# Pairwise products with a projected right factor: pairs ordered by right field, projections in a ring, stores of 100 pairs

## The chip, the cores and the metric

The kernel runs on one core of a Trainium2 chip. The metric is the device time of one execution in microseconds (us), the median of several runs. All transfers between the chip's main memory and the core's on-chip memory (SBUF, 128 partitions) are carried by 16 DMA engines, which take their work from queues: here one fed by the SyncE sequencer (SP) and one fed by the ScalarE sequencer (ACT). TensorE (PE) multiplies matrices into PSUM, ScalarE copies from PSUM to SBUF, VectorE (DVE) does elementwise arithmetic.

## The reference

For a batch of 4096 rows with 32 fields of 64 numbers each, every field is projected by the matrix W, and for each pair of fields i < j the left field is multiplied elementwise with the projected right field. There are 32 x 31 / 2 = 496 pairs, all in fp32:

```python
def _L0_rec_ref(x, W):                      # x (4096, 32, 64), W (64, 64)
    vid = jnp.einsum('bfd,de->bfe', x, W)
    idx_i, idx_j = jnp.triu_indices(32, k=1)
    return x[:, idx_i, :] * vid[:, idx_j, :]   # (4096, 496, 64)
```

The input is 33.6 MB and the output 520 MB, so the output is nearly all of the traffic.

## The kernel before

**Tiles.** The host lays x out as 16 tiles of 128 partitions x 32 fields x 128 numbers. A partition is one of the 64 embedding positions of one of two halves of the batch; the 128 numbers are batch rows. One field of one partition is 512 B, and one pair of one tile is 128 x 512 B = 64 KB of output.

**Loads.** W is loaded twice, onto partitions 0 to 63 and 64 to 127, by two transfers on ACT's queue (L53, L54). x of tile 0 comes in four pieces of 8 fields, last fields first, and x of tile 1 in two pieces of 16 fields, all on SP's queue (L99 to L102; the transfer itself is L61). Later tiles are loaded in four pieces of 8 fields on ACT's queue, one after each of the second to fifth chunks of the tile before (L124, L125). There are two buffers for x, so a load of tile t + 1 waits for the last product of tile t - 1.

**Projection.** `project` (L63) runs over the four groups of 8 fields. Each group takes four fp32 matmul calls of 64 x 64 by 64 x 512 (L72), which come out as eight matmul instructions in the trace, into one of four PSUM buffers, and ScalarE copies the group into `vid` (L79). `vid` is one buffer for all 32 fields of a tile; there are two of them.

**Products and stores.** Pairs are numbered by left field: `off[i]` is the first pair of left field i. The 496 pairs of a tile are cut into chunks of SLOT = 83 pairs (six a tile, the last of 81), each in one of three output buffers. `products` (L82) writes a chunk with one VectorE multiply for each left field in it (L88): the left operand is field i of x, repeated over the right fields; the right operand is a range of `vid`. `store` (L96) then sends the chunk on SP's queue. In tile 0 the chunks run backwards, from the last pair, because the last left fields need only the last fields of `vid`; its first chunk is stored in four parts (10, 18, 27 and 26 pairs) and the others in two (L107 to L117). From tile 1 on each chunk is one store (L119 to L123).

**Order.** SP's instructions stand in the order of the program text. The instructions of the other engines are ordered by the scheduler and wait for each other through semaphores. An output buffer is written again only after its store has landed on all 16 DMA engines.

Of the kernel before, what the change touches and what calls it, by code (L numbers as in the profile page):

```python
# [1 line left out]

# [4 lines left out]

F32 = mybir.dt.float32
ALU = mybir.AluOpType

P = 128

C = 128


@with_exitstack
def pairwise_bilinear_kernel(
    ctx: ExitStack,
    tc: tile.TileContext,
    x: bass.AP,  # L20
    w: bass.AP,
    out: bass.AP,
):

    nc = tc.nc
    NT, _, F, _ = x.shape
    D = P // 2
    NP = F * (F - 1) // 2

    GRP = 8  # L30
    NGRP = F // GRP
    BANK = 512 // C

    SLOT = 83
    AHEAD = 2
    PIECES = 4

    off = [i * (F - 1) - i * (i - 1) // 2 for i in range(F)]


    ctx.enter_context(tc.manual_schedule(engines={mybir.EngineType.SP}))

    const = ctx.enter_context(tc.tile_pool(name="const", bufs=1))
    xpool = ctx.enter_context(tc.tile_pool(name="x", bufs=AHEAD))
    vpool = ctx.enter_context(tc.tile_pool(name="vid", bufs=2))
    opool = ctx.enter_context(tc.tile_pool(name="out", bufs=3))
    psum = ctx.enter_context(
        tc.tile_pool(name="ps", bufs=4, space=bass.MemoryType.PSUM)
    )


    w2 = const.tile([P, D], F32)
    nc.scalar.dma_start(out=w2[0:D, :], in_=w)  # L53
    nc.scalar.dma_start(out=w2[D : 2 * D, :], in_=w)  # L54

    xs = {}

    def load(t, lo, hi, queue=nc.sync):
        if t not in xs:
            xs[t] = xpool.tile([P, F, C], F32, tag="x", name=f"x_{t}")  # L60
        queue.dma_start(out=xs[t][:, lo:hi, :], in_=x[t][:, lo:hi, :])  # L61

    def project(t, order):  # L63

        vid = vpool.tile([P, F, C], F32, tag="vid", name=f"vid_{t}")
        for g in order:
            pv = psum.tile([P, GRP, C], F32, tag="pv", name=f"pv_{t}_{g}")
            for b in range(0, GRP, BANK):
                f = g * GRP + b
                for h in range(2):  # L70
                    half = slice(h * D, (h + 1) * D)
                    nc.tensor.matmul(  # L72
                        pv[half, b : b + BANK, :],
                        lhsT=w2[half, :],
                        rhs=xs[t][half, f : f + BANK, :],
                        start=True,
                        stop=True,
                    )
            nc.scalar.copy(vid[:, g * GRP : (g + 1) * GRP, :], pv)  # L79
        return vid  # L80

    def products(t, vid, ot, base, a, b, backwards=False):  # L82

        fields = [i for i in range(F - 1) if off[i] < b and off[i + 1] > a]
        for i in reversed(fields) if backwards else fields:
            s, e = max(a, off[i]), min(b, off[i + 1])
            j = i + 1 + s - off[i]
            nc.vector.tensor_tensor(  # L88
                ot[:, s - base : e - base, :],
                xs[t][:, i : i + 1, :].to_broadcast([P, e - s, C]),  # L90
                vid[:, j : j + e - s, :],
                ALU.mult,
            )

    def store(t, ot, base, a, b):
        nc.sync.dma_start(out=out[t][:, a:b, :], in_=ot[:, a - base : b - base, :])  # L96


    for g in reversed(range(NGRP)):  # L99
        load(0, g * GRP, (g + 1) * GRP)  # L100
    load(1, F // 2, F)
    load(1, 0, F // 2)  # L102

    for t in range(NT):
        vid = project(t, reversed(range(NGRP)) if t == 0 else range(NGRP))
        bases = list(range(0, NP, SLOT))
        if t == 0:  # L107

            ends = [NP, off[27], off[24], off[21], bases[-1]]
            for n, base in enumerate(reversed(bases)):  # L110
                top = min(base + SLOT, NP)
                if n:
                    ends = [top, (base + top) // 2, base]
                ot = opool.tile([P, SLOT, C], F32, tag="o", name=f"o_{t}_{n}")
                for b, a in zip(ends, ends[1:]):
                    products(t, vid, ot, base, a, b, backwards=True)
                    store(t, ot, base, a, b)  # L117
        else:
            for n, base in enumerate(bases):  # L119
                top = min(base + SLOT, NP)  # L120
                ot = opool.tile([P, SLOT, C], F32, tag="o", name=f"o_{t}_{n}")
                products(t, vid, ot, base, base, top)
                store(t, ot, base, base, top)  # L123
                if 1 <= n <= PIECES and t + 1 < NT and t + 1 not in (0, 1):  # L124
                    load(t + 1, (n - 1) * F // PIECES, n * F // PIECES, nc.scalar)  # L125


_INS = ["r_x", "L0_rec_W"]
_OUTS = [((4096, 496, 64), "float32")]


# [28 lines left out]
```

## Time and profile before

| | |
|---|---|
| median of 3 runs (lowest, highest) | 1298.11 us (1298.02, 1298.69) |
| the profiled execution, its own time | 1297.79 us |
| its span, first to last instruction | 1295.9 us |
| VectorE busy, instructions | 1105.9 us (85%), 581 |
| TensorE busy | 219.4 us (17%) |
| ScalarE busy | 66.1 us (5%) |
| DMA packets, bytes, mean rate over the span | 24077, 553.82 MB, 427 GB/s |
| stores of 83 pairs: number, issue to landing | 75, 28.9 us |
| stores of 81 pairs | 15, 27.6 us |
| x loads of 512 KB on ACT's queue | 56, 31.8 us |
| first product of VectorE starts at | 10.89 us |
| first store is issued at | 12.6 us |

How to read it: a profile page divides the span into 40 slices and gives for each the busy share of every engine and of the DMA engines, then each DMA queue's packets, bytes and the time its packets took as a share of all 16 DMA engines' time. A packet here is one partition's contiguous piece of a transfer. The chain of waits goes back from the last instruction, at each step to what released it. "Landing" is the arrival of a transfer's completion at its semaphore. Each transfer adds one to its semaphore from each of the 16 DMA engines, so the trace also has the moment at which each engine finished its part.

### The profile page before, as it was taken

The page shows a single profiled execution, that of the slowest core. Times are in us where ns is not written, and L with a number is a line of the kernel's source. Part 1 is how long each engine was busy: PE and PEld are TensorE (multiplying, and loading weights), DVE is VectorE, ACT ScalarE, POOL GpSimd, SP SyncE. Part 2 cuts the span into 40 slices and gives each one's busy share as a digit, 9 for nine tenths or more (in the row PEclk, how much of TensorE's full clock was granted, in tenths as well). Part 3 has the DMA queues.
Part 4 walks back from the last instruction along what each step waited for, and adds up shares of the span by engine and source line. Part 5 has one row for each costly group of instructions (what it writes and reads, how often), then busy time and mean ns, then how long its engine had stood idle before and what let it go on. Part 6 is the DMA issues. An engine that isn't in the chain of part 4 may idle for free.

```text
span 1295.9 us, 2185 instructions
## 1 busy us (share of the span) xinstructions
PE 219.4 (17%) x512; PEld 55.2 (4%) x512; DVE 1105.9 (85%) x581; ACT 66.1 (5%) x65; POOL 0.2 (0%) x4
## 2 busy tenths in 40 slices
PE   5013022120221302113031120211203122021000
PEld 2000000000000000000000000000000000000000
DVE  6999988889888888888888888888888888888991
ACT  2001000000000000000000000000000000000000
POOL 0000000000000000000000000000000000000000
PEclk9556556565665556655566555655556555565555
DMA  8999999999999999999999999999999999999998
GB/s 337 430 403 442 433 434 432 430 434 431 431 435 435 431 432 434 433 430 435 432 432 436 432 429 432 433 431 431 434 428 431 439 427 438 430 423 444 430 430 353
DMA packets 24077, 553.82 MB, mean 427 GB/s; under 512 B 2817, under 2 KB 2817, under 8 KB 10625
## 3 DMA queue, kind: packets, MB, share of 16 engines
q1 hardware_dynamic: 15840, 524.30, 93.9%
q10 hardware_dynamic: 8224, 29.40, 5.6%
q8 instruction: 4, 0.07, 0.0%
q14 instruction: 9, 0.07, 0.0%
HBM read 33.59 MB, written 520.09 MB: 427 GB/s over the span
## 4 chain that ended last, share of the span: by engine, by line
DMA 63%; DVE 33%; issue 1%; PE 0%; DVEq 0%; ACT 0%
DMA out_dram<-o 63%; DVE o L88 33%; DMA w<-in_L_rec_W_dram 0%; PE pv L72 0%; DVEq L154 0%; ACT vid L79 0%; DVEq L88 0%
## 5 line engine op out<-in xcount | busy, mean ns | idle before, releaser
L88 DVE TENSOR_TENSOR o<-x,vid 128x1408 f32<-128x1408 f32 (+15 forms) x581 | 1105.9, 1974 | 163.7 <-DMA out_dram<-o 152.9
L72 PE MATMUL pv<-x,w 64*64 64x512 f32 x512 | 219.4, 1002 | 958.4 <-DMA x<-in_r_x_dram 953.1
L79 ACT COPY vid<-pv 128x1024 f32<-128x1024 f32 x64 | 64.8, 1012 | 1110.8 <-PE pv L72 1072.2
L72 PEld LDWEIGHTS pv<-x,w 64*64 64x64 f32 x512 | 55.2, 205 | 1120.9 <-issue 1109.1
L79 ACT ACT_TABLE_LOAD x1 | 1.3, 1283 | 2.0 <-issue 2.0
L139 POOL MEMSET const-bfloat16-1.0<- 128x1 bf16 x1 | 0.1, 101 | 0.0
L139 POOL MEMSET const-uint8-127<- 128x1 uint8 x1 | 0.1, 101 | 0.0
L139 POOL MEMSET const-float32-0.0<- 128x1 f32 x1 | 0.1, 98 | 0.2 <-issue 0.2
L139 POOL MEMSET const-float32-1.0<- 128x1 f32 x1 | 0.1, 98 | 0.0
## 6 DMA issues: line engine op xcount, KB each, us to landing
out_dram<-o SPq DMA_DIRECT2D x75, 5312.0 KB, 28.9
out_dram<-o SPq DMA_DIRECT2D x15, 5184.0 KB, 27.6
x<-in_r_x_dram ACTq DMA_DIRECT2D x56, 512.0 KB, 31.8
out_dram<-o SPq DMA_DIRECT2D x5, 2688.0 KB, 10.2
out_dram<-o SPq DMA_DIRECT2D x5, 2624.0 KB, 10.8
x<-in_r_x_dram SPq DMA_DIRECT2D x4, 512.0 KB, 5.8
x<-in_r_x_dram SPq DMA_DIRECT2D x2, 1024.0 KB, 9.8
out_dram<-o SPq DMA_DIRECT2D x1, 1728.0 KB, 5.5
```

Of the source, the lines that this page charges most:

```text
L72: nc.tensor.matmul(pv[half, b : b + BANK, :], lhsT=w2[half, :], rhs=xs[t][half, f : f + BANK, :], start=True, stop=True,)
L79: nc.scalar.copy(vid[:, g * GRP : (g + 1) * GRP, :], pv)
L88: nc.vector.tensor_tensor(ot[:, s - base : e - base, :], xs[t][:, i : i + 1, :].to_broadcast([P, e - s, C]), vid[:, j : j + e - s, :], ALU ...
L139: nc = _bacc.Bacc("TRN2", target_bir_lowering=False, num_devices=1)
```

## The change

The pairs of a tile are numbered by right field: pair (i, j) is number `first(j) + i` with `first(j) = j (j - 1) / 2`. The outer loop runs over the right field j, and one multiply takes a range of left fields of x and the one projected field j, repeated. The host puts the output's pairs back into the reference's order. A slot holds 100 pairs instead of 83 (five a tile, the last of 96), still with three buffers. `vid` is now one tile per group of 8 fields, in a ring of three buffers, instead of two whole buffers. The scratch space for software-made DMA descriptors is reduced to 1024.

Stores of the first two tiles end where the list GROWING says, and at the end of each slot and tile; after it is used up, each slot is one store. Pairs begin with right field 1 in every tile, so the first products need the first fields, and x of tile 0 is loaded first fields first.

W comes from the host stacked twice, in one transfer, and is the first one on SP's queue. x of tile 0 is loaded in four pieces as before and every later tile in two pieces of 16 fields (8 KB a partition), tiles 0 and 1 on SP and the others on ACT; the load of tile t + 1 stands in the program before the projection of tile t. On ACT it comes to stand behind the copies of groups 0 and 1 of tile t and before those of groups 2 and 3.

```diff
+SLOT = 100
+
+GROWING = [
+    15, 13, 8, 19, 23, 22, 20, 16, 17, 18, 29, 31, 22, 23, 24, 25,
+    53, 22, 35, 61, 55, 45, 71, 29, 76, 24,
+]
+
+def first(j):
+    return j * (j - 1) // 2
...
-    SLOT = 83
-    AHEAD = 2
-    PIECES = 4
...
-    vpool = ctx.enter_context(tc.tile_pool(name="vid", bufs=2))
+    vpool = ctx.enter_context(tc.tile_pool(name="vid", bufs=3))
...
-    nc.scalar.dma_start(out=w2[0:D, :], in_=w)
-    nc.scalar.dma_start(out=w2[D : 2 * D, :], in_=w)
+    nc.sync.dma_start(out=w2, in_=w)
...
+    def load(t, pieces, queue):
+        xt = xpool.tile([P, F, C], F32, tag="x", name=f"x_{t}")
+        n = F // pieces
+        for lo in range(0, F, n):
+            queue.dma_start(out=xt[:, lo : lo + n, :], in_=x[t][:, lo : lo + n, :])
+        return xt
...
+    loaded = [load(0, 4, nc.sync), load(1, 2, nc.sync)]
...
+    for t in range(NT):
+        if 0 < t < NT - 1:
+            loaded.append(load(t + 1, 2, nc.scalar))
+        xt = loaded[t]
...
+            vid.append(vpool.tile([P, GRP, C], F32, tag="vid", name=f"vid_{t}_{g}"))
+            nc.scalar.copy(vid[-1], pv)
...
+        sent = 0
+        for j in range(1, F):
+            i = 0
+            while i < j:
+                at = first(j) + i
+                base = at - at % SLOT
+                if at == base:
+                    ot = opool.tile([P, SLOT, C], F32, tag="o", name=f"o_{t}_{at}")
+                n = min(j - i, base + SLOT - at)
+                nc.vector.tensor_tensor(
+                    ot[:, at - base : at - base + n, :],
+                    xt[:, i : i + n, :],
+                    vid[j // GRP][:, j % GRP : j % GRP + 1, :].to_broadcast([P, n, C]),
+                    ALU.mult,
+                )
+                i += n
+                at += n
+                if t * NP + at == until or at in (base + SLOT, NP):
+                    nc.sync.dma_start(
+                        out=out[t][:, sent:at, :],
+                        in_=ot[:, sent - base : at - base, :],
+                    )
+                    sent = at
+                    if t * NP + at == until:
+                        until += next(growing, NT * NP)
```

## The prediction

> **What bounds the kernel now.** I read the page's slices, queues and chain shares first, then the chain of waits in order of time, then windows over both ends of the span. From the page:
>
> ```profile
> DMA  8999999999999999999999999999999999999998
> ...
> q1 hardware_dynamic: 15840, 524.30, 93.9%
> q10 hardware_dynamic: 8224, 29.40, 5.6%
> ...
> DMA 63%; DVE 33%; issue 1%; PE 0%; DVEq 0%; ACT 0%
> ```
>
> The 16 DMA engines are full in all but the first and last slice. VectorE shows in the chain, but only in turns with a store it waited for. The chain of waits (start, length):
>
> ```profile
> 0.74 4.58 DMA w<-in_L_rec_W_dram
> 5.37 4.45 PE pv L72 x9
> 9.84 1.02 ACT vid L79
> 10.89 13.73 DVE o L88 x15
> ...
> 1102.15 11.79 DVE o L88 x13
> 1113.96 27.52 DMA out_dram<-o
> 1141.58 11.51 DVE o L88 x5
> 1153.11 28.97 DMA out_dram<-o
> 1182.17 11.80 DVE o L88 x13
> ```
>
> A slot comes free, VectorE refills it in 11.5 to 11.8 us, and its store needs 26 to 29 us to land because two others are ahead of it. So the DMA always has work, and one tile takes 1182.17 - 1102.15 = 80.0 us (80.2 on average from 299.48 to 1182.17). Windows (length, five engines' busy time, clock, DMA share, GB/s) show where it has none:
>
> ```profile
> 2.00:3.00 1.00, 0.00 (x0) 0.00 (x0) 0.00 (x0) 1.00 (x1) 0.00 (x0) 1.00 0.87 205
> 3.00:4.00 1.00, 0.00 (x0) 0.00 (x0) 0.00 (x0) 0.24 (x1) 0.00 (x0) 1.00 0.85 226
> ...
> 13.00:14.00 1.00, 1.00 (x7) 0.46 (x4) 1.00 (x2) 0.73 (x1) 0.00 (x0) 1.00 0.74 304
> ...
> 15.00:16.00 1.00, 1.00 (x6) 0.40 (x4) 1.00 (x2) 1.00 (x1) 0.00 (x0) 1.00 0.05 15
> ...
> 18.00:19.00 1.00, 1.00 (x6) 0.40 (x4) 1.00 (x2) 0.58 (x1) 0.00 (x0) 1.00 0.71 295
> 19.00:20.00 1.00, 1.00 (x8) 0.53 (x6) 1.00 (x1) 0.44 (x1) 0.00 (x0) 1.00 0.49 207
> ...
> 28.00:30.00 2.00, 0.00 (x0) 0.00 (x0) 2.00 (x3) 0.00 (x0) 0.00 (x0) 0.50 0.41 172
> ...
> 90.00:100.00 10.00, 5.43 (x13) 1.44 (x15) 10.00 (x5) 1.01 (x1) 0.00 (x0) 0.50 1.03 394
> ```
>
> Against 432 GB/s, the rate of most slices, the loss is: 2.9 us before 4.0, 1 - 304/432 = 0.3 at 13, 1.0 at 15, 0.3 + 0.5 at 18 to 20, 2 x 0.6 = 1.2 at 28 to 30 (3.3 us of gaps between first stores; 3.4 when summed from the single packets), and about 1.2 from 80 to 100. The end loses more: the DMA rate drops to 207 GB/s from 1288 and to 41 by 1291, because the 16 engines do not finish together. By the completion counts of the last store the first is done at 1288.9 and the last at 1295.1; on the first big stores this spread was 1.3 us.
>
> **What the skill says.** The Trainium skill's "DMA: Bandwidth & Descriptors", section "Where 436 GB/s comes from", puts the ceiling at 435.2 GB/s; the packets below give 435. Its section "Issuing engines are not separate DMA queues" says that transfers from ACT and SP share the same 16 engines and interleave; the trace agrees, since a 512 KB load takes 31.8 us to land among stores and 5.8 us at the start. "VectorE: DVE Perf Modes", section "Mode 1x (REGULAR)", gives one result a cycle for fp32 with two tensor operands; the trace has 4291 ns for 3968 elements. "TensorE: Matmul & The Clock Gate", Part 1, has matmuls at half speed for about 3.4 us; here they start 0.43 us apart until about 9.2 and 0.215 after, 3.8 us in.
>
> **The price of a packet.** The two queue rows give two equations: q1 0.939 x 16 x 1295.9 = 19470 us for 524.30 MB in 15840 packets, q10 1161 us for 29.40 MB in 8224. Solved: 36.85 us a MB and 9 ns a packet. The single packets are sharper: 159 ns for 4096 B, 309 for 8192, 1533 for 41,472, 1571 for 42,496, 9 for a completion write, so 8.4 ns + 36.77 ns a KB (of 1000 bytes), 27.2 GB/s an engine. A packet is a row of one partition, and an engine carries 8 rows of each DMA.
>
> **The change, part by part.**
>
> *Fewer packets.* Before, 104 stores, 62 x loads and two of W on half the rows are (104 + 62 + 1) x 8 = 1336 packets an engine and 168 completion writes. After: the GROWING list gives 28 stores in the first two tiles, then 14 tiles x 5 = 70, so 98; 34 loads; 1 W: 133 x 8 = 1064 packets and 133 writes. Saved: 272 x 8.4 = 2.28 us and 35 x 9 = 0.3 us, 2.6 us. A row of 51,200 B does not occur before: on the line it takes 1.891 us. If such rows were cut in two, 57 stores of 100 pairs would give 57 x 8 x 8.4 ns = 3.8 us back, which is the second rival below. The overlap seen in two-queue windows may already hide part of the loads' share, so I bound the saving between 1.2 and 2.8 and take 2.4.
>
> *W first.* One issue on SP (0.44 us a piece there) before the x loads pushes them back by 0.44 us, and with them everything the DMA does. Bounds 0.3 to 1.0, the upper if the slow first reads (2.9 us lost before 4.0) fall on W and again on x. In return PE no longer waits at 5.37 for the first half of W and at 6.76 for the second. x's first piece, landed at 5.16, lands at about 5.6; eight matmuls at the slow rate, 7 x 0.43 + 0.9, end near 9.5; copy 1.02; VectorE starts at about 10.65 instead of 10.89.
>
> *Growing first stores.* VectorE's first operations start 0.21, 0.34, 0.46, 0.61 us apart for 1, 2, 3, 4 pairs: 0.1335 us a pair + 0.065 an operation. Store issue follows the last product by 0.13, the first packet follows the issue by 0.84 (12.62 to 13.46, 15.22 to 16.07). A pair costs the DMA 0.1507 us + 0.07 a store. The loads end at about 13.3 + 0.44 = 13.74. Then, products ready / data could start / DMA done:
> 15 pairs: 12.98 / 13.95 / 16.28, gap 0.2;
> 13: 14.84 / 15.81 / 18.32, none;
> 8: 15.98 / 16.95 / 19.60, none;
> 19: 18.64 / 19.61 / 22.55, 0.01;
> 23: 21.84 / 22.81 / 26.35, 0.26;
> 22: 24.91 / 25.88 / 29.74, none. Carried on in the same way, every later store is ready before the DMA is done with the one ahead; the tightest are the 53 pairs (ready 63.97, DMA busy to 64.39, margin 0.4) and the 61 (80.05, 81.19). The loads of tile 2 then let the lead grow to some 20 us by the end of tile 1. Gaps 0.5 against 3.4: 2.9 us saved, bounds 0 to 3.2.
>
> *The step to full stores.* The 1.2 us lost from 80 to 100 fall where the first load and the first 83-pair store (issued at 92.72, data at 97.39) meet a DMA with little queued. With 55, 45, 71, 29, 76, 24 in its place I take 0.7 back, bounds 0 and 1.4.
>
> *Products by right field, vid ring, slots.* 544 operations instead of 581 on the same elements: 496 x 0.1335 + 34 x 0.065 = 68.4 us a tile, beside 80 of DMA. Cover of a refill: two queued stores of 15.1 us less the engines' spread of 6.2 is 24, against 13.6 + 0.5 + 1.0 us. Cost nothing. The ring: the copies for groups 0 and 1 of a tile take buffers freed before the previous tile ends; groups 2 and 3 stand on ACT behind the two loads of tile t + 1, which wait for the last product of tile t - 1. They issue in about 1.5 us (0.36 + 1.13), the copy takes 1.0, and VectorE asks for it after 120 pairs, 17 us. Loads: 16 rows beside stores of 1.89 us, 16 x 2.2 + 4 = 39 us, wanted 80 us later. On SP each store also waits for the transfer that used its completion semaphore eight earlier, five or more stores back: free.
>
> *End.* The spread of the engines is left at 6.2 us, with 1.5 either way.
>
> Sum: -2.4 + 0.44 - 2.9 - 0.7 = -5.6 us. The profiled execution took 1297.79 us around its span of 1295.9, which gives 1292.2; the median of the runs is 0.3 higher, so 1292.5.
>
> **Rivals.**
>
> *Only the packets are saved.* The gaps reappear: if W first delays x by 1.0 or VectorE starts at 11.3, or a few per cent more per product use up the margins of 0.0 to 0.4 us above. For it: the fourth and fifth store have no margin. Against: a delay of x also moves the end of the loads, so most of it cancels. Time 1298.1 - 2.4 + 0.4 = 1296.1.
>
> *The packets are not saved*, only the head: 1298.1 + 0.4 - 2.9 - 0.7 = 1294.9 if short packets were hidden already, and 3.8 - 2.6 = 1.2 more, 1296.1, if rows of 51,200 B are cut. For it: the share over 1.0 in windows. Against: 309 ns for 8192 B is less than twice 159.
>
> *VectorE becomes the bound.* The broadcast operand is now the second one, vid, and the ranged one x. No row before shows this form. If the second port's repeated reads cost more, the place is every product; the DMA hides up to 80.0 / 68.4, 17% more. Past it the tile follows VectorE: at 25% more, 496 x 0.167 + 2.2 = 85 us, 16 x 85 + 11 + a last store of some 20 = 1391. Against: one operand is broadcast before too, at one element a cycle.
>
> **How the numbers follow.** Chances: forecast 0.72 (its own range 1289.3 to 1295.5), packets only 0.15, head only 0.06, VectorE bound 0.07. Low end: all good bounds at once give -2.8 + 0.3 - 3.2 - 1.4 = -7.1 and a shorter end; 1289.3. High end 1296.6, past the second case. What a measurement can tell from no change is 0.2%, 2.6 us: faster is below 1295.5. Faster, in the order of the cases, 0.69 + 0.06 + 0.04 = 0.79; same 0.13; slower 0.08.
>
> **What would show it.** Packets near 19,200 instead of 24,077; share of the two queues down by 0.2 points; a tile in 79.8 to 80.1 us in the chain; 15:16 and 28:30 at over 400 GB/s; the first product near 10.65 and first store issue near 13.1; mean VectorE time near 2.10 us over 544 (the one before, 1974 ns, less its share of 37 short operations). Wrong would be: a busy VectorE above 1150 us, idle of VectorE put down to ACT at tile starts, gaps after the fourth or fifth store, or a spread at the end beyond 8 us.

## The result: slower by 0.36%

The changed kernel takes 1302.76 us (median of 4 runs, 1301.58 to 1304.48), the kernel before 1298.07 us. The ratio is 1.0036, 95% interval [1.0019, 1.0054]. The forecast was 1292.5 us, faster. The profiled execution took 1304.48 us, the slowest of the four; its span is 1302.7 us.

The rate by slices of the kernel before:

```profile
GB/s 337 430 403 442 433 434 432 430 434 431 431 435 435 431 432 434 433 430 435 432 432 436 432 429 432 433 431 431 434 428 431 439 427 438 430 423 444 430 430 353
```

From the page of the changed kernel (slices of DMA share and rate, packets, queues):

```profile
DMA  9999999999999999999999999999999999999996
GB/s 361 423 425 442 419 437 432 435 445 432 428 436 424 428 434 426 433 444 431 431 425 436 422 432 427 444 421 440 429 432 426 437 422 428 431 425 445 426 431 259
DMA packets 19164, 553.82 MB, mean 425 GB/s; under 512 B 2256, under 2 KB 2256, under 8 KB 3152
...
q1 hardware_dynamic: 15120, 524.33, 93.7%
q10 hardware_dynamic: 4032, 29.36, 5.3%
```

The packets fell as counted, from 24077 to 19164. The first slice rose from 337 to 361 GB/s. The last fell from 353 to 259: the visible loss is at the end. Windows over the start of the changed kernel (length, five engines' busy time, clock, DMA share, GB/s):

```profile
13.00:14.00 1.00, 1.00 (x6) 0.30 (x4) 1.00 (x2) 0.96 (x1) 0.00 (x0) 1.00 0.64 270
14.00:15.00 1.00, 1.00 (x8) 0.42 (x6) 1.00 (x2) 0.34 (x1) 0.00 (x0) 1.00 0.65 270
15.00:16.00 1.00, 1.00 (x8) 0.33 (x6) 1.00 (x2) 0.68 (x1) 0.00 (x0) 1.00 0.99 407
...
19.00:20.00 1.00, 1.00 (x6) 0.30 (x4) 1.00 (x2) 0.00 (x0) 0.00 (x0) 1.00 1.04 414
...
28.00:30.00 2.00, 0.00 (x0) 0.00 (x0) 2.00 (x2) 1.01 (x1) 0.00 (x0) 0.50 0.99 411
90.00:100.00 10.00, 4.21 (x10) 1.37 (x12) 10.00 (x7) 0.45 (x1) 0.00 (x0) 0.50 0.97 417
```

The gaps at 15, 19 and 28 us are gone. One of 0.7 us is left at the first store, at 13 to 15. I call the price of a packet the time that the line of the prediction gives it (8.4 ns and 36.77 ns per 1000 bytes; 9 ns for a completion). By 140 us the packets moved had a price of 131.7 us an engine before the change and of 135.0 us after it, so the engines had lost 8.3 and 5.0 us each. Now the same kind of windows over the end, first before the change:

```profile
1286.00:1288.00 2.00, 0.00 (x0) 0.00 (x0) 0.00 (x0) 0.00 (x0) 0.00 (x0) 0.50 0.91 394
1288.00:1290.00 2.00, 0.00 (x0) 0.00 (x0) 0.00 (x0) 0.00 (x0) 0.00 (x0) 0.50 0.48 207
1290.00:1292.00 2.00, 0.00 (x0) 0.00 (x0) 0.00 (x0) 0.00 (x0) 0.00 (x0) 0.50 0.24 104
1292.00:1294.00 2.00, 0.00 (x0) 0.00 (x0) 0.00 (x0) 0.00 (x0) 0.00 (x0) 0.50 0.10 41
```

and then after it:

```profile
1284.00:1286.00 2.00, 0.00 (x0) 0.00 (x0) 0.00 (x0) 0.00 (x0) 0.00 (x0) 0.50 0.91 394
1286.00:1288.00 2.00, 0.00 (x0) 0.00 (x0) 0.00 (x0) 0.00 (x0) 0.00 (x0) 0.50 0.46 197
1288.00:1290.00 2.00, 0.00 (x0) 0.00 (x0) 0.00 (x0) 0.00 (x0) 0.00 (x0) 0.50 0.34 147
1290.00:1292.00 2.00, 0.00 (x0) 0.00 (x0) 0.00 (x0) 0.00 (x0) 0.00 (x0) 0.50 0.28 123
1292.00:1294.00 2.00, 0.00 (x0) 0.00 (x0) 0.00 (x0) 0.00 (x0) 0.00 (x0) 0.50 0.28 123
1294.00:1296.00 2.00, 0.00 (x0) 0.00 (x0) 0.00 (x0) 0.00 (x0) 0.00 (x0) 0.50 0.23 98
1296.00:1298.00 2.00, 0.00 (x0) 0.00 (x0) 0.00 (x0) 0.00 (x0) 0.00 (x0) 0.50 0.06 25
1298.00:1300.00 2.00, 0.00 (x0) 0.00 (x0) 0.00 (x0) 0.00 (x0) 0.00 (x0) 0.50 0.06 25
```

A share of 0.28 is four or five of the 16 DMA engines, 0.06 is one. By the completion counts of the last store, twelve engines are done between 1287.8 and 1290.8, and four at 1296.1, 1297.5, 1298.1 and 1301.3. Before, fourteen were done within 3.6 us, the last 6.2 us after the first. So the program waits at the end for a few engines that fell behind.

I call the time from the first to the last engine's completion of one store the spread. It stays near 0.2 us up to 80 us, in both kernels, and then grows from tile to tile: in the changed kernel 0.55 at 240 us, 6.0 at 598, 11.6 at 923, 16.5 at 1151. It grows almost only while a tile's loads are under way: the three stores complete at 598, 613 and 628 us all have 6.0, then two loads land, and the stores at 679, 695 and 710 us all have 7.7. After the last load, landed at 1154 us, it no longer grows: 14.4 at 1167, 13.5 at the end.

The chain of waits shows what the lag costs in the middle of the run:

```profile
1115.66 14.40 DVE o L103 x14
...
1130.08 36.58 DMA out_dram<-o
...
1166.75 13.71 DVE o L103 x4
...
1180.47 31.46 DMA out_dram<-o
```

A slot is free when the slowest engine has stored it. The lengths of these waits say little: three slots of 15.1 us less a refill of 14 us give 31 us from issue to landing, and the load rows of a tile add up to 4.9. The pace says more. The same fill came round in the chain at 384.64, 628.27, 872.43 and 1115.66, three tiles apart: 81.1 to 81.4 us a tile, where the forecast had 79.8 to 80.1 and the price of a tile's packets is 80.05.

### The profile page after: what moved, and what is told of

Same layout as the page of the kernel before. It is cut to its first block, busy times and chain, and to the rows that moved or that the text cites. A ratio compares the mean times of both kernels' runs of the same rounds, so it can differ in the third digit from the quotient of the medians.

```text
span 1302.7 us, 2118 instructions
## 1 busy us (share of the span) xinstructions
PE 184.5 (14%) x512; PEld 55.3 (4%) x512; DVE 1101.7 (85%) x544; ACT 66.1 (5%) x65; POOL 0.2 (0%) x4
## 2 busy tenths in 40 slices
DMA packets 19164, 553.82 MB, mean 425 GB/s; under 512 B 2256, under 2 KB 2256, under 8 KB 3152
## 4 chain that ended last, share of the span: by engine, by line
DMA 62%; DVE 31%; issue 1%; DVEq 0%
DMA out_dram<-o 62%; DVE o L103 31%; DVEq L149 0%; DVEq L103 0%
## 5 line engine op out<-in xcount | busy, mean ns | idle before, releaser
L103 DVE TENSOR_TENSOR o<-x,vid 128x1280 f32<-128x1280 f32 (+27 forms) x544 | 1101.7, 2098 | 168.2 <-DMA out_dram<-o 157.0
L84 PE MATMUL pv<-x,w 64*64 64x512 f32 x512 | 184.5, 886 | 975.7 <-DMA x<-in_r_x_dram 975.7
## 6 DMA issues: line engine op xcount, KB each, us to landing
out_dram<-o SPq DMA_DIRECT2D x2, 1856.0 KB, 13.6
```

What stands on the lines that cost most here:

```text
L84: nc.tensor.matmul(pv[half, b : b + BANK, :], lhsT=w2[half, :], rhs=xt[half, g + b : g + b + BANK, :], start=True, stop=True,)
L103: nc.vector.tensor_tensor(ot[:, at - base : at - base + n, :], xt[:, i : i + n, :], vid[j // GRP][:, j % GRP : j % GRP + 1, :].to_broadcas ...
```

## The experiments

Spreads below are those of the last store in the profiled execution of each run. Each is from one execution, so a difference of one or two microseconds says little.

**1. Which part makes the engines lag?** Candidates were the load rows (8 KB, 4 KB before: theory L) and the store rows (51,200 B, 42,496 B before: theory S). Four kernels cross the two.

Changed kernel, later loads in four pieces (a_load4k):

```diff
-            loaded.append(load(t + 1, 2, nc.scalar))
+            loaded.append(load(t + 1, 4, nc.scalar))
```

> The changed kernel with the x loads of tiles 2 to 15 in four pieces of 8 fields (4 KB rows) instead of two (8 KB rows); 56 loads on ACT again. The trace of the changed kernel shows its first gaps closed and its packets down, but three or four DMA engines finish 10 to 13 us after the other twelve. Theory L (8 KB load rows beside stores make some engines fall behind): the spread of the engines at the last store falls from 13.6 to about 6 us and the time to about 1293 to 1295 us. Theory S (the larger stores of 51,200 B rows do it): the spread stays at 11 to 15 us and the time at 1302 to 1304.

Changed kernel, slots of 83 pairs, with a growing list that ends on them (a_slot83):

```diff
-SLOT = 100
+SLOT = 83
```

> The changed kernel with slots of 83 pairs (stores of 42,496 B rows) and a list of growing stores that ends on them; loads stay at 8 KB rows. Theory S (large store rows do it): spread about 6 us, time 1293 to 1296. Theory L (8 KB load rows do it): spread 11 us or more, limited by the smaller slots (two stores of 12.6 us less a refill of 13 us leave some 12 us of lag before the fast engines run dry), time 1300 or more.

Kernel before, later loads in two pieces (b_load8k):

```diff
-    PIECES = 4
+    PIECES = 2
```

> The kernel before with its x loads of tiles 2 to 15 in two pieces of 16 fields (8 KB rows). Theory L: the spread at the last store grows from 6.2 to 10 us or more and the time rises from 1298.1 to 1301 to 1305. Theory S: spread stays near 6, and the time falls by the packets saved, about 2 us, to 1296.

Both edits to the changed kernel (a_slot83_load4k):

> The changed kernel with slots of 83 pairs and 4 KB load rows: what is left of the change is the head (W first, pairs by right field, growing stores) and the vid ring. If L or S or both together are the cause, the spread is about 6 us and the time 1298.1 + 0.4 - 3 = about 1295. If the time stays at 1302 the cause is neither, but the order of the loads on ACT, the pair layout or the memory layout (theory O).

| kernel | store row, load row | median us | ratio to before, 95% | spread us |
|---|---|---|---|---|
| before | 42,496 B, 4 KB | 1298.19 | 1 | 6.2 |
| changed | 51,200 B, 8 KB | 1302.76 | 1.0036 [1.0019, 1.0054] | 13.5 |
| a_load4k | 51,200 B, 4 KB | 1296.33 | 0.9983 [0.9974, 0.9991] | 8.2 |
| a_slot83 | 42,496 B, 8 KB | 1312.35 | 1.0095 [1.0064, 1.0126] | 11.0 |
| b_load8k | 42,496 B, 8 KB | 1304.37 | 1.0045 [1.0030, 1.0060] | 11.5 |
| a_slot83_load4k | 42,496 B, 4 KB | 1297.30 | 0.9993 [0.9984, 1.0001] | 7.0 |

Theory L holds and S falls. The load row alone moves the changed kernel by 6.4 us and the kernel before by 6.2 us, and smaller store rows do not bring the spread down: with 8 KB load rows it stays at 11, and the time goes up to 1312. The profiled execution of that kernel was its fastest run, 1303.84, so its trace doesn't show the 1312, and why the smaller slots cost so much stays open. a_load4k came out 1 to 3 us above its forecast, its spread 8.2 and not 6; a_slot83_load4k came out 2 us above its own, and it removes theory O.

The end of a_load4k, for comparison with the windows above:

```profile
1284.00:1286.00 2.00, 0.00 (x0) 0.00 (x0) 0.00 (x0) 0.00 (x0) 0.00 (x0) 0.50 0.51 221
1286.00:1288.00 2.00, 0.00 (x0) 0.00 (x0) 0.00 (x0) 0.00 (x0) 0.00 (x0) 0.50 0.34 147
1288.00:1290.00 2.00, 0.00 (x0) 0.00 (x0) 0.00 (x0) 0.00 (x0) 0.00 (x0) 0.50 0.17 74
1290.00:1292.00 2.00, 0.00 (x0) 0.00 (x0) 0.00 (x0) 0.00 (x0) 0.00 (x0) 0.50 0.11 49
1292.00:1294.00 2.00, 0.00 (x0) 0.00 (x0) 0.00 (x0) 0.00 (x0) 0.00 (x0) 0.50 0.00 0
```

The tail has the same form, but the last engine is done at 1293.5 us, 7.9 us earlier. Not all of that is spread: the first engine too is done earlier, at 1285.3 us instead of 1287.8, though this kernel has more packets. The account of the prediction below comes back to it.

**2. What in the load row: its length, its pitch in memory, the number of transfers, or the alternation of two queues?** All four start from the changed kernel.

Eight pieces of 2 KB rows (`load(t + 1, 8, nc.scalar)`, a_load2k):

> The changed kernel with the x loads of tiles 2 to 15 in eight pieces of 4 fields (2 KB rows, 112 loads). Theory L1 (the shorter a load row, the less the stores beside it are held up): the excess of large store packets over their length falls below that with 4 KB rows (26 us, against 88 with 8 KB), spread at the last store 3 to 6 us, time 1293 to 1296 although 14 x 32 packets an engine more cost 3.8 us of every engine. Theory L2 (4 KB is as good as it gets; only rows over 4 KB hold stores up): spread as with 4 KB, 7 to 8 us, time 1298 to 1300.

Rows 16,896 B apart (a_pitch):

```diff
+    x = _np.pad(x, ((0, 0), (0, 0), (0, 1), (0, 0)))
...
     NT, _, F, _ = x.shape
+    F -= 1
```

> The changed kernel, loads of 8 KB rows, but with a spare field behind the 32 of each partition in main memory, so that the rows lie 16,896 B apart and not 16,384. Theory H (rows a power of two apart meet in the memory and hold some engines up): spread below 6 us, time 1291 to 1294. Theory Q (the hold-up comes from the alternation of a load row and a store row on an engine, wherever the row comes from): unchanged, spread 11 us or more, 1301 to 1304.

Two loads a tile as in the change, cut into rows of 4 KB by the layout in memory, those of tile 1 too (a_cut4k):

```diff
-    NT, _, F, _ = x.shape
+    NT, G, _, F, _ = x.shape
+    F *= G
...
-            queue.dma_start(out=xt[:, lo : lo + n, :], in_=x[t][:, lo : lo + n, :])
+            queue.dma_start(
+                out=xt[:, lo : lo + n, :].rearrange("p (g f) c -> p g (f c)", f=F // G),
+                in_=x[t, lo * G // F : (lo + n) * G // F].rearrange("g p f c -> p g (f c)"),
+            )
...
+    x = x.reshape(NT, 2 * D, 4, F // 4, C).transpose(0, 2, 1, 3, 4)
```

> The changed kernel with two loads a tile as in the change, but with x laid out in main memory group by group, so that each load consists of rows of 4 KB, two to a partition (also for tile 1). If the length of a row decides: as with four loads of 4 KB rows, 1295 to 1297, spread 6 to 9. If the number or size of the transfers decides: as the change, 1301 to 1304, spread over 11.

Loads on SP's queue (a_spload):

```diff
-        if 0 < t < NT - 1:
-            loaded.append(load(t + 1, 2, nc.scalar))
...
+                    if at == SLOT and 0 < t < NT - 1:
+                        loaded.append(load(t + 1, 2, nc.sync))
```

> The changed kernel with the two 8 KB-row loads of tile t + 1 put on SP's queue, behind the first full slot's store of tile t, so that one queue carries everything and an engine never alternates between two. Theory Q (alternation between the queues holds up the stores): excess of large store packets near the level outside load windows, spread below 4 us, time 1289 to 1293. If reading from memory beside writing is what costs, on any queue: spread over 10, 1300 or more. A new wait would show as VectorE idle put down to ACT or PE at tile starts.

| kernel | median us | ratio, 95% | spread us |
|---|---|---|---|
| a_load2k | 1332.21 | 1.0260 [1.0243, 1.0278] | 1.6 |
| a_pitch | 1300.78 | 1.0024 [1.0015, 1.0033] | 13.5 |
| a_cut4k | 1295.57 | 0.9980 [0.9972, 0.9988] | 6.9 |
| a_spload | 1303.65 | 1.0044 [1.0029, 1.0059] | 13.6 |

The pitch of the rows is not it, as far as one other pitch can tell (spread unchanged, against theory H), nor the number of transfers (a_cut4k has two loads a tile and behaves like a_load4k), nor the alternation of two queues (theory Q falls). a_load2k met neither of its forecasts and answered another question. Its chain of waits:

```profile
483.89 36.95 DMA x<-in_r_x_dram
...
521.24 15.38 another core or an unknown queue
...
536.68 27.58 DMA out_dram<-o
```

On each engine a load row took turns with a store row: in a_load4k the load rows of a tile are spread over 61 us on average, where 32 turns would take 66. 64 load rows a tile beside store rows of 1.891 us need 64 x (1.891 + 0.084) = 126 us (0.084 from the packet line), and a tile has 80. The loads come too late, and stores wait for them: the transfers use eight completion semaphores in rotation, and a store is issued only when the transfer that used its semaphore before has landed. SP's queue waited 589 us for loads here, and not at all in the changed kernel. With 32 rows of 4 KB the count of turns is 66 us, which fits into a tile. The small spread here can't be compared with the others: by 1200 us the times of an engine's packets added up to 22.9 us less than the clock, in the changed kernel to no less.

**3. No loads, longer rows, and short rows without turns.** Without the loads of tiles 2 to 15 (a_noload):

```diff
-            loaded.append(load(t + 1, 2, nc.scalar))
+            loaded.append(loaded[t - 1])
```

> The changed kernel without the loads of tiles 2 to 15: these tiles use the x of tile 0 or 1 again, so 14 x 2 loads are left out, 14 x (16 x 0.309 + 2 x 0.009) = 69.5 us of every engine. If the load rows beside the stores cause the whole lag: spread at the last store 1 to 4 us, excess of large store packets under 10 us, and a span of 1302.7 - 69.5 - about 9 = 1224. If stores of 51,200 B rows lag by themselves: spread over 8 us, span 1231 to 1235.

One load of 16 KB rows (`load(t + 1, 1, nc.scalar)`, a_load16k):

> The changed kernel with one load a tile of 16 KB rows. If the hold-up grows with the row (26 us of excess in store packets with 4 KB rows, 88 with 8 KB): over 100 us of excess, but the lag is cut off by the slots (two stores of 15.1 us less a refill of 15 us: 15 us), so time 1303 to 1310. If it is set by the number of bytes read or by 8 KB or more: as the change, 1301 to 1304.

Edits of a_cut4k and a_spload together (a_cut4k_sp), and the same with rows of 2 KB (a_cut2k_sp):

> The changed kernel with both edits: x in main memory in rows of 4 KB, two to a partition and load, and the two loads of a tile on SP's queue behind the first full slot's store. If only the row length counts: as with 4 KB rows on ACT's queue, 1295 to 1296.5, spread about 7. If the alternation of two queues adds something to it: 1292 to 1294, spread below 5.

> As the run before it, with rows of 2 KB (four to a partition and load, also for tiles 0 and 1): 64 packets an engine and tile instead of 32, 14 x 32 x 8.4 ns = 3.8 us more for every engine. On SP's queue they cannot fall behind the stores as the eight loads of 2 KB rows on ACT's queue did. If the hold-up keeps falling with the row: spread 2 to 4 us, time 1295 to 1297 (3 won at the end, 4 lost in packets). If it doesn't: spread 7, time 1299 to 1301.

| kernel | median us | ratio, 95% | spread us |
|---|---|---|---|
| a_noload | 1223.69 (one run, span 1221.9) | | 1.7 |
| a_load16k | 1302.48 | 1.0040 [1.0024, 1.0056] | 10.7 |
| a_cut4k_sp | 1302.49 | 1.0033 [1.0026, 1.0040] | 12.3 |
| a_cut2k_sp | 1298.56 | 1.0004 [0.9995, 1.0012] | 7.2 |

Without loads there is no lag, with the large stores as they are. That goes against S once more, and the span is 2 us from the forecast. But "the shorter row, the less lag" is only half of it. 4 KB rows on SP's queue, where the 32 rows of a tile are read one after the other (5.1 us of reading), lag about as much as 8 KB rows (12.3). On ACT's queue the same rows take turns with stores, over 59 us of each tile on average, and lag 6.9. I had expected at most 1296.5 for it by either theory and measured 1302.49. Of 4 KB and 2 KB on SP's queue, the shorter lags less (7.2; forecast 2 to 4 or 7). So the length of a row counts, and for 4 KB rows so does the queue. That it is the turns that help is my reading and not shown: a_spload takes the turns away from 8 KB rows too, and there the spread stays the same (13.6 and 13.5). 16 KB rows were not worse than 8 KB ones; of the two forecasts for them, the one of over 1303 failed.

In these traces the longer times lie in packets during the loads. With loads on ACT's queue it is store rows: those of 51,200 B, 1891 ns as a rule, took up to 0.75 us more, most of it between the first load row and the last. With loads on SP's queue it is mostly the load rows themselves: 8 KB rows, 309 ns as a rule, took up to 1.4 us in a_spload. The sum of such excess alone is no measure of the lag, though: over all engines the large store rows have 53 us of it in a_noload against 88 in the changed kernel. But in a_noload three quarters of them are a few ns longer and only 19 by more than 50 ns; in the changed kernel 418 are.

**4. Which side of the load: the read of main memory, the write into SBUF, or a short row between long ones?** All three have no loads for tiles 2 to 15, which use the x of tile 0 or 1 again, and instead two transfers a tile of 8 KB rows at the place of a_spload's, into a buffer that nobody reads. From SBUF to SBUF, with slots of 83 pairs to make room (f_sbuf), from SBUF to main memory (f_write), from main memory to main memory (f_dram). The common edit, with `xt` or `x[t + 1]` as the source:

```diff
+                    if at == SLOT and 0 < t < NT - 1:
+                        for lo in (0, F // 2):
+                            nc.sync.dma_start(
+                                out=scratch[:, lo : lo + F // 2, :],
+                                in_=xt[:, lo : lo + F // 2, :],
+                            )
```

> The kernel without the loads of tiles 2 to 15 (they use x of tile 0 or 1 again), slots of 83 pairs to make room, and on SP's queue, at the place of the loads of a run above, two copies a tile of the same 8 KB rows from SBUF to SBUF; the copies are not used. If reading main memory is what makes some engines lag: spread at the last store 1 to 3 us. If any transfer into SBUF beside stores, or a short row between long ones, does it: spread over 8 us.

> The kernel without the loads of tiles 2 to 15 and, at their place on SP's queue, two copies a tile of 8 KB rows from SBUF to a spare buffer in main memory. If reading main memory is the cause: spread 1 to 3 us. If short rows between long ones are, whatever their direction: spread over 8 us.

> The kernel without the loads of tiles 2 to 15 and, at their place on SP's queue, two copies a tile of 8 KB rows from x in main memory to a spare buffer in main memory, so that nothing is written into SBUF. If reading main memory beside the stores is the cause: spread over 8 us, as with the loads on SP's queue (13.6). If writing into SBUF beside the stores' reads is: 1 to 3 us.

| kernel | reads main memory | writes SBUF | us (one run; before 1298.31) | spread us |
|---|---|---|---|---|
| f_sbuf | no | yes | 1295.04 | 1.4 |
| f_write | no | no | 1293.78 | 1.6 |
| f_dram | yes | no | 1304.24 | 12.8 |
| a_spload (above) | yes | yes | 1303.65 | 13.6 |

The read of main memory beside the stores is what makes some engines fall behind. The same bytes in the same rows at the same place, written to main memory and not read from it, leave the engines together. The rows themselves show it too: no 8 KB row of the copies in f_write took more than 0.34 us, and those in f_dram took up to 1.68. The smaller slots of f_sbuf do not explain its spread, since a_slot83 has them too and has 11.0. The end of f_write:

```profile
1286.00:1288.00 2.00, 0.00 (x0) 0.00 (x0) 0.00 (x0) 0.00 (x0) 0.00 (x0) 0.50 1.08 467
1288.00:1290.00 2.00, 0.00 (x0) 0.00 (x0) 0.00 (x0) 0.00 (x0) 0.00 (x0) 0.50 0.17 74
1290.00:1292.00 2.00, 0.00 (x0) 0.00 (x0) 0.00 (x0) 0.00 (x0) 0.00 (x0) 0.50 0.00 0
```

All engines stop within two microseconds. The end of f_dram, by contrast, has the tail of the changed kernel:

```profile
1290.00:1292.00 2.00, 0.00 (x0) 0.00 (x0) 0.00 (x0) 0.00 (x0) 0.00 (x0) 0.50 0.28 123
1292.00:1294.00 2.00, 0.00 (x0) 0.00 (x0) 0.00 (x0) 0.00 (x0) 0.00 (x0) 0.50 0.28 123
1294.00:1296.00 2.00, 0.00 (x0) 0.00 (x0) 0.00 (x0) 0.00 (x0) 0.00 (x0) 0.50 0.06 25
1296.00:1298.00 2.00, 0.00 (x0) 0.00 (x0) 0.00 (x0) 0.00 (x0) 0.00 (x0) 0.50 0.06 25
1298.00:1300.00 2.00, 0.00 (x0) 0.00 (x0) 0.00 (x0) 0.00 (x0) 0.00 (x0) 0.50 0.06 25
```

What stays open is why the reads hit three or four engines most and not all alike, and which ones: a packet in the trace carries no engine number, and no run moved rows to other engines.

Two versions beat both kernels, the one before by 0.2%: the change with load rows of 4 KB, as four loads (a_load4k, 0.9983 [0.9974, 0.9991]) or as two loads with the rows cut by the layout (a_cut4k, 0.9980 [0.9972, 0.9988]).

## Why the prediction was wrong, step by step

**The bound** was read right. The DMA engines set the time before and after, and VectorE, at 1101.7 us busy over 544 operations of 2098 ns (forecast 2.10), never did. The third rival, in which the repeated second operand costs VectorE more, did not happen.

**W first**: the first piece of x was complete at 6.3 us, not 5.6, and 1.15 us later than before: the slow first reads fell on x again, and the delay went a little past the upper bound of that step. All eight matmuls of the first group then ran at the slow rate, starting at 6.44. The first product came at 11.20 (forecast 10.65, before 10.89) and the first store was issued at 13.66 (forecast 13.1). It cost little, because the loads were also still running.

**Growing first stores and the step to full ones**: 8.3 us lost by 140 us became 5.0. That is 3.3 us less, where the sum had -2.9 - 0.7 + 0.44 = -3.2. The parts were +0.6 up to 13 us, -2.6 from there to 80 us and -1.3 from 80 to 140, so the close agreement of the sum is in part luck.

The steps that failed lie behind 140 us. By how much each one missed shows when the last store's completion is taken for the mean of the 16 engines and for the last one, with the loss against the price of the packets beside it (all in us, from the profiled executions):

| kernel | price of all packets | lost by 140 | lost by 1200 | mean engine complete | last engine complete |
|---|---|---|---|---|---|
| before | 1285.2 | 8.3 | 5.5 | 1290.8 | 1295.1 |
| changed | 1282.6 | 5.0 | 7.8 | 1290.9 | 1301.3 |
| b_load8k | 1283.0 | 8.4 | 10.5 | 1293.7 | 1302.0 |
| a_load4k | 1284.7 | 4.5 | 2.7 | 1287.6 | 1293.5 |
| f_write | 1282.6 | 5.1 | 6.9 | 1289.9 | 1291.0 |

The forecast moved every engine by -5.6, and in these executions the last one moved by +6.3, a miss of 11.9 us. The mean engine did not move, which is 5.7 us of the miss, and the last engine fell 10.4 us behind the mean instead of 4.3, which is the other 6.2.

**The larger failure is the last step, "The spread of the engines is left at 6.2 us, with 1.5 either way"**. The spread came out at 13.5. I had treated the 16 DMA engines as one resource whose packets add up; the time is set by the slowest of them. The profile before held the sign: the spread there grew from 0.2 us at 80 us over 1.3 at the first big stores to 6.2 at the end, and a thing that grows through the run has a cause in every tile. I took it for a constant of the chip and did not ask which part of a tile made it. Had I asked, the loads were the only traffic that the change altered in kind. Against the kernel before, this step alone makes the change slower.

**The other failure is "Fewer packets", the 2.4 us.** The count was right (19164, forecast near 19,200), and so was the row of 51,200 B at 1891 ns: the price fell by 2.6 us. But 2.1 of these belong to the load rows, and load rows did not cost their price. Between 140 and 1200 us the kernel before won 2.8 us back against the price: in these 1060 us its packets took 1064 us an engine, so some of them overlapped. The changed kernel lost 2.8 us more in the same stretch. That the load row makes this difference is shown by b_load8k: 2.2 us less price than the kernel before, and a mean engine 2.9 us later. The second rival, in which short packets were hidden already, had this part right, and its evidence, shares above 1.0 in the windows, was on the page. That 4 KB rows are hidden because they take turns with store rows is not shown: a_cut4k takes the same turns and won only 0.1 us in that stretch.

f_write, which moves the same bytes in the same rows with no reads beside the stores, took 1293.78 us, 1.3 us above the forecast. That nearness is luck and confirms no sum: its spread is 1.6 where the forecast had 6.2, and its mean engine is 1.0 us earlier than the one before where the forecast had 5.6.

My own fast-case rivals were wrong in the same place: both left the end alone. The range ended at 1296.6 because no case in it let the engines drift apart, though a spread beyond 8 us was named among the signs of error.

## What to carry to other kernels

When the DMA engines are the bound, look at each engine's completions and not only at their mean: ask whether the spread of a store's completions grows along the run, and what in each tile feeds it. Larger load rows save packets (8.4 ns each by price here), but here that saving did not reach the mean engine, and reads of main memory beside a stream of stores made a few engines fall behind, by 11 to 14 us in all with 8 KB rows and 6 to 8 with 4 KB rows on a queue of their own. Before the pieces are made smaller, count the turns: 64 load rows an engine beside store rows of 1.9 us did not fit into a tile of 80 us, and that kernel was 34 us slower than the one before.

## What the runs showed of the hardware

- A row of one partition took 8.4 ns plus 36.77 ns a 1000 bytes on its DMA engine, from 4096 to 51,200 B.
- The lag of single engines came from reading main memory beside stores. SBUF to SBUF and SBUF to main memory in the same rows left a spread of 1.4 and 1.6 us, main memory to main memory 12.8.
- The same 4 KB rows lagged 12.3 us when read in one go on the stores' queue and 6.9 when they came from a second queue and took turns with store rows. For 8 KB rows the queue made no difference (13.6 and 13.5).
- Two loads a tile of 8 KB rows instead of four of 4 KB rows saved 2.2 us of packets by price in the kernel before, and its mean engine was complete 2.9 us later.
- Rows 16,384 or 16,896 B apart made no difference to the spread (13.5 in both).
